# A graph-attention layer on one core: halves written straight from PSUM, second halves a step later, two turned tiles at once, remainders on GpSimd

## The chip, the core and the metric

The kernel runs on one core of one Trainium2 chip. A core has five engines that run their own instruction streams side by side: TensorE (PE in the profile; PEld are its weight loads), VectorE (DVE), ScalarE (ACT), GpSimd (POOL) and SyncE (SP). SP mainly issues DMAs; ACT and POOL can issue some as well. Every engine takes its instructions in the order in which they were issued to it. An instruction whose input isn't ready waits on a semaphore, and everything behind it on the same engine waits too. Working tiles lie in SBUF; TensorE writes its results to PSUM, whose banks hold 512 fp32 values in each of 128 partitions. A tile that is used again may be written only when all readers of its old content are done.

The metric is the device time of one execution in microseconds (us). Lower is better.

## What is computed

One pre-norm attention layer over a graph of 384 nodes with 1024 features and 16 heads of 64, all in fp32:

```python
h = jnp.maximum(_layernorm(x, axis=-1), 0.0)
q = h @ wq.T + bq ;  k = h @ wk.T + bk ;  v = h @ wv.T + bv
q2 = (q @ wiq.T + biq).reshape(N, H, D).transpose(1, 0, 2)
k2 = (k @ wik.T + bik).reshape(N, H, D).transpose(1, 0, 2)
v2 = (v @ wiv.T + biv).reshape(N, H, D).transpose(1, 0, 2)
mask = _build_mask(edge_index, edge_type, edge_type_weights, x.dtype)
scores = jnp.einsum('hnd,hmd->hnm', q2, k2) * scale + mask[None]
attn = jax.nn.softmax(scores, axis=-1)
out = jnp.einsum('hnm,hmd->hnd', attn, v2)
out = out.transpose(1, 0, 2).reshape(N, OUT_F)
return x + out @ wo.T + bo
```

The mask is a table of 384 by 384, filled from 6528 edges: minus infinity where there is no edge, the softplus of a weight by edge type where there is one.

## The kernel before

**Numbers in two parts.** To keep fp32 accuracy, an operand is held as a high part (`hi`, rounded) and a remainder (`lo`, the operand less `hi`), and a product is three matmuls into the same bank, hi·hi, hi·lo and lo·hi (`mm3`, L373 to L376, the rows L374, L375, L376 of the profile). Weights come by DMA into `raw` (`load`, L64); `split_hi` (L71, the row L81 on ACT or L79 on DVE) makes the high part and `split_lo` (L83, the row L86, on DVE or POOL) the remainder. One chunk of weights is 128 by 1024.

**Stages.** First comes the layernorm: three row tiles are normalized and turned by TensorE, eight transposes a tile in two groups of four (`ln_transpose`, L289; row L295), which ACT and DVE evict (L302, L304, L309); `warm` (L312) fills PE before that. Then come the projections v, q, iv and k, 8 chunks each of 24 matmuls. Beside them POOL and DVE build the mask table, until about 150 us.

**The fused attention loop** (L825 to L855) has 48 steps of score tiles and 11 more to drain. A step i handles score tile i, that is head i//3 and row tile i%3, at several stages of a pipeline, and issues in this order: matmuls of a filler (below), the scores `do_S(i)` (L705; two matmuls, row L711), more filler, then

- `do_ttr(i-1)` (L713, row L717, DVE): adds the mask and takes the row minimum, straight from PSUM into a tile `e`
- `do_low(i-4)` (L746, row L748, DVE) and later `do_high(i-3)` (L742, row L744, ACT), for row tile 0 of each head only (`DT = (0,)`): the normalized probabilities in fp16 as high part and remainder, which `do_turn` (L750) turns by a transposing DMA on SP's queue
- `do_exp(i-2)` (L719, row L721, ACT): exponential with its row sum
- `do_norm(i-3)` (L732): the reciprocal of the sum on DVE (L734), and for row tiles 1 and 2 the product with it on POOL (L738)
- `turns_and_av` (L777): in every third step the six transposes of row tiles 1 and 2 of a head (`turn_mm`, L755, row L758, into two PSUM banks `t`) alternate with the six matmuls of probabilities and values of the head before (`av_mm`, L769, row L773, into bank `a`)
- `do_pt` (L761), a step later, for each of the two turned tiles: ACT writes the fp16 high part (L766), DVE the remainder (L767)
- `do_ao` (L786): ACT moves one 64-partition half of the attention output (L793), DVE adds the other (L794); for each pair of heads `do_aos` (L796) splits the output into two parts, the high one on ACT (L798) and the remainder on POOL (L799)
- `run_tasks`: the head of the next chunk of the filler, and `wo_prep` (L639) in the steps of `WSTEPS`: split and load of a chunk of the output weights.

**The filler** gives PE work between the scores: `fill` (L804) takes matmuls from a list at 7.9 to 8 a step. First `fill_qk` (L610): the second projections of q and k, 16 chunks ("iq" and "ik", one pair for each two heads), which run just ahead of the heads that need them. `qk_head` (L599) starts a chunk: it evicts the previous one (`qk_done`), splits the weights of the chunk after next (its remainder on POOL for odd chunks, `PAR = 1`) and loads a further one. `qk_done` (L571) evicts a 128 by 384 result into a staging tile `nat` as high part (ACT, L384) and remainder (DVE, L385); eight DMAs for each pair of chunks then copy it by 64-partition halves into the stacks `qs` and `ks`. A stack holds, for one head, high part and remainder on top of each other, so that one matmul over 128 partitions does two of the three products, and a second one the third.

Then `fill_o` (L672): the output projection, six blocks `a` (row tile, column half), each summed over eight chunks `k` in two parts (k 0 to 3, then 4 to 7) in a bank `g` or `s`. When a part is complete, `ysum` (L660, row L663 on DVE) adds the bank to the result tile `res`. It is issued only when the bank is claimed for the next block:

```python
if k == 0:
    flush_y(1)
    oacc[OT[a]] = bank("g")
```

The order of the first part is written out by hand in `first` (L675); `wready[k]` and `6 * k + OREADY` say from which step a block may be taken.

**The end** (L862 to L874): k=7 of five blocks, each with its sum and store, then the last block in two column halves, each in a bank `t`.

`bank` (L48) takes PSUM tiles of one bank from a pool: three `g`, one `a`, two `s`, two `t`, which are all eight banks.

Of the kernel before, what the change touches and what calls it, by code (L numbers as in the profile page):

```python
# [26 lines left out]
def gnn_kernel(ctx: ExitStack, tc: tile.TileContext, x, edges, erows, etw, wq, wk, wv, wiq, wik, wiv, wo,  # L27
# [19 lines left out]

    def bank(tag):  # L48
        return psum.tile([128, 512], F32, tag=tag, name=tag, bufs={"g": 3, "a": 1}.get(tag, 2))
# [201 lines left out]
    rrow = work.tile([128, 2, N], F32R, tag="qs", name="rrow").bitcast(F32)[:, 0, :]  # L251
# [131 lines left out]
    def evac(ps, hi, lo, bias):  # L383
        nc.scalar.activation(hi, ps[:, :N], AF.Identity, bias=bias)  # L384
        nc.vector.scalar_tensor_tensor(lo, ps[:, :N], bias, hi.bitcast(F32), op0=OP.add, op1=OP.subtract)  # L385

# [75 lines left out]
    def residual(k):  # L462

        if k == 0:
            t = work.tile([128, 2, 2, N], F32R, tag="ks", name="bot")
            bob["b"] = t.bitcast(F32).rearrange("p a k n -> p (a k n)")[:, 0:D]
            nc.sync.dma_start(bob["b"], bo.partition_broadcast(128))
        if 1 <= k < 4:
            nc.sync.dma_start(xb[k - 1], x[(k - 1) * 128:k * 128, :])

    def residual_add(i):
        y = res[:, i // 2, i % 2 * 512:i % 2 * 512 + 512]
        nc.gpsimd.tensor_tensor(y, y, bob["b"][:, i % 2 * 512:i % 2 * 512 + 512], OP.add)
# [45 lines left out]
    def v2_early():  # L519
        t = work.tile([128, 2, N], F32R, tag="nat", name="tv", bufs=2)  # L520
        tv = t.bitcast(F32).rearrange("p a n -> p (a n)")[:, :512]
        nc.scalar.activation(tv, accs[5], AF.Copy)
        accs[5] = tv
# [45 lines left out]
    gps = {}  # L569

    def qk_done(w):  # L571
        n, p = chunks[w]
        q2 = nc.scalar if p == 0 else nc.sync
        nat = work.tile([128, 2, N], F32R, tag="nat", name="nat", bufs=2)
        evac(gps[w], nat[:, 0, :], nat[:, 1, :], bc[:, (3 if n == "iq" else 4) * 8 + p:(3 if n == "iq" else 4) * 8 + p + 1])
        nf = nat.bitcast(F32)
        if n == "iq":
            qs = work.tile([128, 2, N], F32R, tag="qs", name="qs")
            qf = qs.bitcast(F32)
            nc.sync.dma_start(qf[0:64, 0, :], nf[0:64, 0, :])  # L580
            q2.dma_start(qf[64:128, 0, :], nf[0:64, 1, :])
            nc.sync.dma_start(qf[0:64, 1, :], nf[64:128, 1, :])
            q2.dma_start(qf[64:128, 1, :], nf[64:128, 0, :])
            stacks["q", p] = qs
        else:
            ks = work.tile([128, 2, 2, N], F32R, tag="ks", name="ks")
            kf = ks.bitcast(F32)
            for o in range(2):
                for r in range(2):
                    (q2 if r else nc.sync).dma_start(kf[r * 64:(r + 1) * 64, o, :, :], nf[o * 64:(o + 1) * 64, :, :])  # L590
            stacks["k", p] = ks

    tasks = []
# [5 lines left out]
    def qk_head(w):  # L599
        if pendq:  # L600
            pendq.pop(0)()
        if 0 < w - W0 < NTAB:
            mask_select(w - W0)
        split_hi(w + 2)
        split_lo(w + 2, nc.gpsimd if (w + 2) % 2 == PAR else None)
        load(w + 5)
        if w == W0:
            mask_select(0)
# [21 lines left out]
    DT = (0,)  # L630
    PRE, RATE, RATE_O, RATE_E = 84, 7.9, 8, 8
    WSTEPS = (37, 40, 42, 44, 47, 51)
    PAR, OPOOL, ODVE = 1, (2, 3, 4, 6), (2,)
# [5 lines left out]
    def wo_prep(k):  # L639

        dst = None
        if k == 4:
            otile[0] = gtile("g3").rearrange("p a k n -> p (a k n)")
        if 4 <= k < 7:
            g, b = otile[0], (k - 4) * 2048
            dst = (g[:, b:b + 1024], g[:, b + 1024:b + 2048])
        split(WO + k, nc.gpsimd if k in OPOOL else None, dst, k in ODVE)
        load(WO + k + 3)
# [23 lines left out]
    def fill_o():  # L672


        first = [(0, 0), (0, 1), (1, 0), (1, 1), (2, 0), (2, 1)]  # L675
        first += [(a, k) for k in (2, 3) for a in range(3)] + [(a, k) for a in range(3, 6) for k in range(KH)]
        for a, k in first:
            while now[0] < wready[k] or now[0] < 6 * k + OREADY:
                yield 0
            if k == 0:  # L680
                flush_y(1)
                oacc[OT[a]] = bank("g")
# [5 lines left out]
        todo = [(a, k) for k in range(KH, 7) for a in range(5)]  # L688
        while todo:
# [6 lines left out]
            if k == KH:  # L696
                flush_y(1)
                oacc[OT[a]] = bank("gggss"[a])
# [3 lines left out]
    st_ps, es, sts, tps, avs, aof = {}, {}, {}, {}, {}, {}  # L702
    S = 48

    def do_S(i):  # L705
        h, t = divmod(i, 3)
        p, o = divmod(h, 2)
        qs, ks = stacks["q", p], stacks["k", p]
        ps = st_ps[i] = bank("s")
        for s in range(2):  # L710
            nc.tensor.matmul(ps[:, :N], qs[:, o, t * 128:(t + 1) * 128], ks[:, o, s, :], start=(s == 0), stop=(s == 1))  # L711

    def do_ttr(i):  # L713
        t = i % 3
        e = es[i] = work.tile([128, N], F32, tag="e", name="e", bufs=EB)
        s = sts[i] = work.tile([128, 4], F32, tag="s", name="s", bufs=12)
        nc.vector.tensor_tensor_reduce(e, st_ps.pop(i)[:, :N], ma[:, t, :], -0.125, 3.0e38, OP.add, OP.min, s[:, 0:1])  # L717

    def do_exp(i):  # L719
        s = sts[i]  # L720
        nc.scalar.activation(es[i], es[i], AF.Exp, bias=s[:, 0:1], scale=-1.0, accum_out=s[:, 1:2])  # L721
# [9 lines left out]

    def do_norm(i):  # L732
        s = sts[i]
        nc.vector.reciprocal(s[:, 2:3], s[:, 1:2])  # L734
        if i % 3 in DT:
            nc.vector.tensor_scalar(s[:, 2:3], s[:, 2:3], PSC, None, op0=OP.mult)
        else:
            nc.gpsimd.tensor_tensor(es[i], es[i], s[:, 2:3].to_broadcast([128, N]), OP.mult)  # L738

    planes = {}  # L740

    def do_high(i):  # L742
        planes[i] = plv[i // 3 % 3]
        nc.scalar.activation(planes[i][:, 0, :], es[i], AF.Copy, scale=sts[i][:, 2:3])  # L744

    def do_low(i):  # L746
        pl = planes[i]
        nc.vector.scalar_tensor_tensor(pl[:, 1, :], es.pop(i), sts[i][:, 2:3], pl[:, 0, :], op0=OP.mult, op1=OP.subtract)  # L748
# [6 lines left out]
    def turn_mm(i):  # L755
        ps = tps[i] = bank("t")
        for k in range(3):
            nc.tensor.transpose(ps[:, k * 128:(k + 1) * 128], es[i][:, k * 128:(k + 1) * 128], ident)  # L758
            yield

    def do_pt(i):  # L761
        h, t = divmod(i, 3)
        pt = ptv[h % 3]
        hi, lo = (pt[:, s * 3:s * 3 + 3, t * 128:(t + 1) * 128] for s in range(2))
        pv = tps.pop(i)[:, :N].rearrange("p (k n) -> p k n", k=3)
        nc.scalar.activation(hi, pv, AF.Copy, scale=PSC)  # L766
        nc.vector.scalar_tensor_tensor(lo, pv, PSC, hi, op0=OP.mult, op1=OP.subtract)  # L767
# [18 lines left out]
    def do_ao(h):  # L786
# [7 lines left out]
        nc.vector.scalar_tensor_tensor(aof[p][m, :], ps[m, :N], down[m], tmp[m, :], op0=OP.mult, op1=OP.add)  # L794
# [26 lines left out]
    for h in range(16):  # L821
        for t in (1, 2):
            t_at.setdefault(3 * h + 7 if h < 15 else 3 * h + 5 + t, []).append(3 * h + t)
        a_at[3 * h + 10 if h < 15 else 3 * h + 9] = h
    for i in range(S + 11):  # L825
# [8 lines left out]
        if 0 <= i - 4 < S and (i - 4) % 3 in DT:  # L834
# [3 lines left out]
        if 0 <= i - 3 < S:  # L838
            do_norm(i - 3)
            if (i - 3) % 3 in DT:  # L840
                do_high(i - 3)
        turns_and_av(t_at.get(i, []), [a_at[i]] if i in a_at else [])
        for x in t_at.get(i - 1, []):
            do_pt(x)
        if i - 1 in a_at:
            do_ao(a_at[i - 1])
        if a_at.get(i - 2, 0) % 2:
            do_aos(a_at[i - 2])
        run_tasks()
        if 0 <= i - 4 < S and (i - 4) % 3 in DT:  # L850
            do_turn(i - 4)
        if i in WSTEPS:
            wo_prep(wp)
            wready[wp] = i + 2
            wp += 1  # L855
    while gens:
# [57 lines left out]
```

## Time and profile before

| what | value |
|---|---|
| median of 3 runs | 296.02 us (294.78 to 296.08) |
| the profiled execution | 294.56 us, span 292.8 us |
| granted TensorE clock | 1.00 |
| PE busy | 284.7 us, 97% of the span, 1610 matmuls |
| VectorE busy | 208.2 us, 71% |
| ScalarE busy | 159.7 us, 55% |
| GpSimd busy | 154.8 us, 53% |
| from 180 to 200 us: PE, VectorE, ScalarE, GpSimd busy | 20.00, 15.13, 16.51, 10.65 us |
| from 250 to 260 us: PE busy | 8.88 of 10 us |
| stacks filled by SP's DMAs (q2 and k2) | 30 of 96 KB and 30 of 192 KB |

The span is the time from the first to the last instruction seen by the profiler; the 1.76 us beside it lie around it. A line of the timeline or of the groups gives a start or a total, a duration, the engine, the line of the code, the operation, output and inputs with their shapes, how often, and in brackets how long the engine had been idle and for whom. A line of the waits says which instruction of which engine waited for which, in all, how many times, and the longest. PE's matmul records overlap (the ends are modelled), so the distance between two starts is the better measure of what a matmul costs.

From 184 to 206 us the heads follow each other at equal distance: the transposes of successive heads start at 185.63, 192.49 and 199.33 us.

### The profile page before, as it was taken

Reading aid. Unit: us, or ns where it says so; the run is one execution under the profiler, and the core shown is the slowest. Engines: PE = TensorE matmul, PEld = TensorE weight load, DVE = VectorE, ACT = ScalarE, POOL = GpSimd, SP = SyncE. Lnnn points to the kernel's source line nnn. Section 1 sums busy time; section 2 is a strip of 40 time slices with the busy share of each in tenths; the row PEclk is TensorE's granted clock in tenths of the full one; section 3 lists DMA queues with packets and bytes.
Section 4 is the critical chain, followed back from the end, with each engine's and each line's share of the span. In section 5 each row is a group of like instructions: output and inputs, shape, how many; then the busy total and the mean of one; then the engine's idle time right before and its main releaser. Section 6 shows DMA issues by size and latency. Waiting matters only on the chain. (4 is left out here: it accounts for less than half of the span.)

```text
span 292.8 us, 4859 instructions
## 1 busy us (share of the span) xinstructions
PE 284.7 (97%) x1610; PEld 267.4 (91%) x1610; DVE 208.2 (71%) x509; ACT 159.7 (55%) x291; POOL 154.8 (53%) x153
## 2 busy tenths in 40 slices
PE   6999999999999999999999999999999999989995
PEld 5999999999988889999999999999999998868874
DVE  3858996667665452999966768878786876788623
ACT  3894543244331222343643778787878788766510
POOL 3765576437775787992004256262627268636210
PEclk9999999999999999999999999999999999999999
DMA  7799857973463342278438879879797969901105
GB/s 268 248 321 404 292 209 254 323 242 112 143 189 122 121 146 72 72 224 296 154 86 227 241 208 211 212 166 227 166 234 147 254 133 234 230 2 27 27 3 215
DMA packets 33305, 54.60 MB, mean 187 GB/s; under 512 B 17408, under 2 KB 20992, under 8 KB 33280
## 3 DMA queue, kind: packets, MB, share of 16 engines
q1 hardware_dynamic: 30896, 51.90, 61.4%
q0 software_dynamic: 2064, 1.80, 2.2%
q10 hardware_dynamic: 320, 0.59, 0.8%
q8 instruction: 13, 0.21, 0.3%
q14 instruction: 12, 0.10, 0.1%
HBM read 38.30 MB, written 3.39 MB: 142 GB/s over the span
## 5 line engine op out<-in xcount | busy, mean ns | idle before, releaser
L374 PE MATMUL g<-g,whl 128*128 128x384 f32 x312 | 105.8, 339 | 0.0
L376 PE MATMUL g<-g,whl 128*128 128x384 f32 x312 | 104.3, 334 | 0.0
L375 PE MATMUL g<-g,whl 128*128 128x384 f32 x312 | 104.2, 334 | 0.0
L231 POOL DMA_INDIRECT tab<-val,idx x51 | 59.7, 1171 | 32.0 <-issue 11.8
L81 ACT ACTIVATE whl<-raw 128x1024 fp32r<-128x1024 f32 x51 | 53.5, 1050 | 29.8 <-PE g L376 21.1
L86 DVE TENSOR_TENSOR whl<-raw,whl 128x1024 fp32r<-128x1024 f32 x41 | 53.8, 1313 | 20.1 <-ACT whl L81 17.0
L374 PEld LDWEIGHTS g<-g,whl 128*128 128x128 f32 x312 | 58.6, 188 | 0.2
L375 PEld LDWEIGHTS g<-g,whl 128*128 128x128 f32 x312 | 58.6, 188 | 0.0
L376 PEld LDWEIGHTS g<-g,whl 128*128 128x128 f32 x312 | 58.6, 188 | 0.1
L390 ACT ACTIVATE g<-f,bc 128x384 fp32r<-128x384 f32 x24 | 14.8, 618 | 53.7 <-DVE f L389 44.8
L738 POOL TENSOR_TENSOR e<-e,s 128x384 f32<-128x384 f32 x32 | 26.4, 829 | 31.2 <-DVE s L734 23.0
L86 POOL TENSOR_TENSOR whl<-raw,whl 128x1024 fp32r<-128x1024 f32 x11 | 26.3, 2395 | 25.9 <-ACT whl L81 25.0
L721 ACT ACTIVATE e<-e,s 128x384 f32<-128x384 f32 x48 | 29.1, 607 | 2.0 <-DVE s L717 1.2
L717 DVE CUSTOM_DVE_ANT_0 e<-s,ma 128x384 f32<-128x384 f32 x48 | 26.4, 552 | 4.3 <-PE s L711 3.7
L389 DVE TENSOR_TENSOR f<-g,rrow 128x384 f32<-128x384 f32 x24 | 13.3, 554 | 18.0 <-PE g L376 18.0
L773 PE MATMUL a<-pt,vhl 128*128 128x384 f16 x96 | 26.1, 326 | 0.0
L758 PE MATMUL t<-ident,e 128*128 128x128 f32 x96 | 24.9, 272 | 0.0
L711 PE MATMUL s<-ks,qs 128*128 128x384 f32 x96 | 24.5, 335 | 0.0
L767 DVE SCALAR_TENSOR_TENSOR pt<-t,pt 128x384 f16<-128x384 f32 x32 | 16.6, 549 | 8.2 <-ACT pt L766 8.2
L799 POOL TENSOR_TENSOR g<-aof,g 128x384 fp32r<-128x384 f32 x8 | 8.3, 1041 | 25.5 <-ACT g L798 25.5
L711 PEld LDWEIGHTS s<-ks,qs 128*128 128x128 f32 x96 | 17.5, 188 | 0.9
L744 ACT ACTIVATE pt<-e,s 128x384 f16<-128x384 f32 x16 | 9.9, 616 | 15.4 <-issue 9.4
(166 smaller groups left out, 447.0 us busy)
## 6 DMA issues: line engine op xcount, KB each, us to landing
ks<-nat SPq DMA_DIRECT2D x30, 192.0 KB
raw<-in_wv_dram SPq DMA_DIRECT2D x8, 512.0 KB
raw<-in_wq_dram SPq DMA_DIRECT2D x8, 512.0 KB
raw<-in_wiv_dram SPq DMA_DIRECT2D x8, 512.0 KB
raw<-in_wk_dram SPq DMA_DIRECT2D x8, 512.0 KB
raw<-in_wiq_dram SPq DMA_DIRECT2D x8, 512.0 KB
raw<-in_wik_dram SPq DMA_DIRECT2D x8, 512.0 KB
raw<-in_wo_dram SPq DMA_DIRECT2D x8, 512.0 KB
```

The costliest lines, as they stand in the source:

```text
L81: nc.scalar.activation(dst[0], raw[w], AF.Copy)
L86: (eng or nc.vector).tensor_tensor(lo, raw[w], hi.bitcast(F32), OP.subtract)
L231: nc.gpsimd.indirect_dma_start(out=tabs[c // RNG], out_offset=bass.IndirectOffsetOnAxis(ap=idx[:, c:c + 1], axis=0), in_=val[:, c:c + 1], ...
L374: nc.tensor.matmul(ps, lhi, rhi, start=first, stop=False)
L375: nc.tensor.matmul(ps, lhi, rlo, start=False, stop=False)
L376: nc.tensor.matmul(ps, llo, rhi, start=False, stop=last)
L711: nc.tensor.matmul(ps[:, :N], qs[:, o, t * 128:(t + 1) * 128], ks[:, o, s, :], start=(s == 0), stop=(s == 1))
L717: nc.vector.tensor_tensor_reduce(e, st_ps.pop(i)[:, :N], ma[:, t, :], -0.125, 3.0e38, OP.add, OP.min, s[:, 0:1])
L721: nc.scalar.activation(es[i], es[i], AF.Exp, bias=s[:, 0:1], scale=-1.0, accum_out=s[:, 1:2])
L738: nc.gpsimd.tensor_tensor(es[i], es[i], s[:, 2:3].to_broadcast([128, N]), OP.mult)
L758: nc.tensor.transpose(ps[:, k * 128:(k + 1) * 128], es[i][:, k * 128:(k + 1) * 128], ident)
L773: nc.tensor.matmul(ps[:, :N], vhl[:, k, h, :, :], ptv[h % 3][:, 3 * s + k, :], start=(k == 0 and s == 0), stop=(k == 2 and s == 1))
```

## The change

- **One PSUM tile for the turned tiles.** The two banks `t` become one tile `turn` of two banks. `bank("t")` gives its halves in turn. `turn_mm` writes both turned tiles of a head side by side into it, and `do_pt` evicts both with one instruction on ACT and one on DVE (head 15, whose tiles are turned in two steps, keeps two).
- **Stacks from PSUM.** `qk_done` writes the two 64-partition halves of q2 and k2 from PSUM into the stacks, high part by ACT and remainder by DVE, each half by itself. The staging tile and its DMAs go. Only the high part of k2, which is needed on both halves of the partitions, is copied by a DMA, one for each head; the unused quarter of the k stacks is set to zero once, by POOL.
- **VectorE's second halves a step later.** The remainders of `qk_done` and `do_pt`, the second half of `do_ao` and those remainders of the output weights that are on DVE go to a list `later`, which is run in the next step just behind `do_ttr`. `do_aos` comes a step later too, and the loop has one step more.
- **Remainders on GpSimd.** The remainders of all second-projection chunks (and of the first two chunks of the output weights) go to POOL.
- **Output projection.** `flush_y` runs at the end of every step. `first` takes the blocks k = 0, 1 of the first three banks and then k = 2, 3 of them bank by bank, `todo` takes block 2 after 3 and 4, and two entries of `WSTEPS` are earlier (36 and 38 for 37 and 40).
- The row sums and factors of a head lie in one small tile, with some generality that is not used (`LAG = 0`).

```diff
+    turn = psum.tile([128, 2, 512], F32, tag="t", name="t", bufs=1)
+    nturn = itertools.count()
+
     def bank(tag):
-        return psum.tile([128, 512], F32, tag=tag, name=tag, bufs={"g": 3, "a": 1}.get(tag, 2))
+        if tag == "t":
+            return turn[:, next(nturn) % 2, :]
+        return psum.tile([128, 512], F32, tag=tag, name=tag, bufs={"g": 3, "a": 1, "s": 2}[tag])
...
+    ksb = [[work.tile([128, 2, N], F32R, tag=f"ks{o}", name="ks") for j in range(2)] for o in range(2)]
+    for o in range(2):
+        for j in range(2):
+            nc.gpsimd.memset(ksb[o][j].bitcast(F32)[64 - o * 64:128 - o * 64, 1, :], 0.0)
 
     def qk_done(w):
         n, p = chunks[w]
-        q2 = nc.scalar if p == 0 else nc.sync
-        nat = work.tile([128, 2, N], F32R, tag="nat", name="nat", bufs=2)
-        evac(gps[w], nat[:, 0, :], nat[:, 1, :], bc[:, (3 if n == "iq" else 4) * 8 + p:(3 if n == "iq" else 4) * 8 + p + 1])
...
+        for o in range(2):
+            m, l = slice(o * 64, o * 64 + 64), slice(64 - o * 64, 128 - o * 64)
+            if n == "iq":
+                t = work.tile([128, N], F32R, tag=f"qs{o}", name="qs", bufs=2 + o)
+                hi, lo = t[m, :], t[l, :]
+            else:
+                t = ksb[o][p % 2]
+                hi, lo = t[m, 0, :], t[m, 1, :]
+            stacks[n, p, o] = t
+            nc.scalar.activation(hi, ps[m, :N], AF.Identity, bias=bias[m])
+            halves.append((m, hi, lo))
+            if n == "ik":
+                kf = t.bitcast(F32)
+                (nc.scalar if p == 0 and o else nc.sync).dma_start(kf[l, 0, :], kf[m, 0, :])
+        for m, hi, lo in halves:
+            later.append(lambda m=m, hi=hi, lo=lo: nc.vector.scalar_tensor_tensor(
+                lo, ps[m, :N], bias[m], hi.bitcast(F32), op0=OP.add, op1=OP.subtract))
+        if now[0] < 0:
+            run_later()
...
-        split_hi(w + 2)
-        split_lo(w + 2, nc.gpsimd if (w + 2) % 2 == PAR else None)
+        split_hi(w + 2, dve=(w + 2) % 2 == PAR)
+        eng = nc.gpsimd
+        if eng is None and now[0] >= 0:
+            later.append(lambda: split_lo(w + 2))
+        else:
+            split_lo(w + 2, eng)
...
-    WSTEPS = (37, 40, 42, 44, 47, 51)
-    PAR, OPOOL, ODVE = 1, (2, 3, 4, 6), (2,)
+    WSTEPS = (36, 38, 42, 44, 47, 51)
+    PAR, OPOOL, ODVE = 9, (2, 3, 4, 6), (2,)
...
-        split(WO + k, nc.gpsimd if k in OPOOL else None, dst, k in ODVE)
+        split_hi(WO + k, dst, k in ODVE)
+        if k in OPOOL:
+            split_lo(WO + k, nc.gpsimd)
+        else:
+            later.append(lambda: split_lo(WO + k))
...
-        first = [(0, 0), (0, 1), (1, 0), (1, 1), (2, 0), (2, 1)]
-        first += [(a, k) for k in (2, 3) for a in range(3)] + [(a, k) for a in range(3, 6) for k in range(KH)]
+        first = [(a, k) for c in (0, 2) for a in range(3) for k in (c, c + 1)]
+        first += [(a, k) for a in range(3, 6) for k in range(KH)]
...
             if k == 0:
-                flush_y(1)
                 oacc[OT[a]] = bank("g")
...
-        todo = [(a, k) for k in range(KH, 7) for a in range(5)]
+        todo = [(a, k) for k in range(KH, 7) for a in (0, 1, 3, 4, 2)]
...
     def turn_mm(i):
-        ps = tps[i] = bank("t")
+        h, t = divmod(i, 3)
+        ps = turn.rearrange("p b n -> p (b n)")
         for k in range(3):
-            nc.tensor.transpose(ps[:, k * 128:(k + 1) * 128], es[i][:, k * 128:(k + 1) * 128], ident)
+            nc.tensor.transpose(ps[:, k * 256 + (t - 1) * 128:k * 256 + t * 128], es[i][:, k * 128:(k + 1) * 128], ident)
             yield
...
+    def do_pt(x):
+        h, t = divmod(x[0], 3)
+        c = slice(t * 128, (t + len(x)) * 128)
+        hi, lo = (ptv[h % 3][:, s * 3:s * 3 + 3, c] for s in range(2))
+        pv = turn.rearrange("p b n -> p (b n)")[:, :768].rearrange("p (k n) -> p k n", k=3)[:, :, c.start - 128:c.stop - 128]
         nc.scalar.activation(hi, pv, AF.Copy, scale=PSC)
-        nc.vector.scalar_tensor_tensor(lo, pv, PSC, hi, op0=OP.mult, op1=OP.subtract)
+        later.append(lambda: nc.vector.scalar_tensor_tensor(lo, pv, PSC, hi, op0=OP.mult, op1=OP.subtract))
...
-        nc.vector.scalar_tensor_tensor(aof[p][m, :], ps[m, :N], down[m], tmp[m, :], op0=OP.mult, op1=OP.add)
+        dst = aof[p][m, :]
+        later.append(lambda: nc.vector.scalar_tensor_tensor(dst, ps[m, :N], down[m], tmp[m, :], op0=OP.mult, op1=OP.add))
...
-    for i in range(S + 11):
+    for i in range(S + 12):
...
             do_ttr(i - 1)
+        run_later()
...
-        if a_at.get(i - 2, 0) % 2:
-            do_aos(a_at[i - 2])
+        if a_at.get(i - 3, 0) % 2:
+            do_aos(a_at[i - 3])
...
+        flush_y()
```

## The prediction, made before the changed kernel was run

> **What bounds the kernel now.** I read the page first. Its rows of busy time and of slices say that TensorE works 97% of the span and is short of full only in the first slice and near the end:
>
> ```profile
> PE 284.7 (97%) x1610; PEld 267.4 (91%) x1610; DVE 208.2 (71%) x509; ACT 159.7 (55%) x291; POOL 154.8 (53%) x153
> PE   6999999999999999999999999999999999989995
> ```
>
> No other engine is near that, and the granted clock is 1.00 in every stretch. The change issues the same matmuls (1610 rows) in almost the same order, so it can move the end only through the moments in which PE stands still. The view of waits lists them for PE, longest in total first:
>
> ```profile
> PE s L295 <- ACT g L283: 1.5, 1, 1.5
> PE g L315 <- POOL ident masks.py:199: 1.4, 1, 1.4
> PE g L374 <- DVE res L663: 1.4, 1, 1.4
> PE g L295 <- DVE g L287: 0.4, 1, 0.4
> ```
>
> Three of the four are in the layernorm at the start. The third lies in the attention phase, and the timeline there tells what it is:
>
> ```profile
> 258.27 1.23 DVE L86 TENSOR_TENSOR g<-raw,g 128x1024 fp32r<-128x1024 f32 x1 [0.46 <-ACT g L81]
> 258.37 0.51 PE L711 MATMUL s<-ks,qs 128*128 128x384 f32 x2
> 259.51 0.69 DVE L663 TENSOR_TENSOR res<-g,res 128x512 f32<-128x512 f32 x1
> ...
> 260.25 0.50 PE L374 MATMUL g<-whl,g 128*128 128x512 f32 x1 [1.37 <-DVE res L663]
> ```
>
> The output projection needs a bank that ysum (L663) must empty. ysum was only issued when the bank was claimed, and stood on DVE behind a weight remainder (L86) of 1.23 us, which itself had waited for ACT. The second L711 started about 0.17 after 258.37, the next matmul at 260.25: 1.71 between starts that lie 0.17 apart elsewhere, so 1.54 us is lost. Then I read the starts of the other PE rows from 21 us on: outside this place, and 0.11 at 283.33, they follow each other at their own rates.
>
> **The change, part by part.**
>
> *The bank.* flush_y now runs at the end of every step, and the blocks for k=2,3 of bank 0 come before those of bank 1, so the first sum is issued at step 41 and its bank claimed at 43. A step is a third of a head, 6.84/3 = 2.28 us; two steps are 4.56, against 0.69 for ysum and at most the 1.23 of a remainder that may stand before it. The whole 1.54 goes; if DVE is 2.6 us late, it stays. Term: -1.54, bounds -1.54 and 0. wo_prep moves with it (steps 36 and 38 for 37 and 40; hi, remainder on POOL and one 512 KB load each). Transposes of step 19 start at 199.33, so step 38 runs from 242.6 to 244.9; its hi (1.05) and remainder (2.39) then end by 246.0 to 248.3, and k=3 is first read in step 41, at 249.5: 1.2 or more hide it.
>
> *The second use of one PSUM tile, at the start.* The two t banks are now halves of one tile, and the order of the changed program with its waits shows two new PE waits outside the attention. In the layernorm the four transposes of the second t half must now also wait for ACT's eviction of the first:
>
> ```profile
> 8.60 0.59 ACT L302 ACTIVATE g<-t 128x512 fp32r<-128x512 f32 x1
> 8.95 0.60 PE L295 MATMUL t<-ident,g 128*128 128x128 f32 x4
> 9.65 0.59 ACT L302 ACTIVATE g<-t 128x512 fp32r<-128x512 f32 x1
> 10.12 1.16 ACT L351 ACTIVATE whl<-raw 128x512 fp32r<-128x512 f32 x2
> ```
>
> The eviction ends at 9.19, so with about 0.1 for the release the transposes start at 9.25 to 9.30 instead of 8.95. They end 0.60 later, at 9.9; ACT, which began at 9.65, follows 0.3 later, then L351, the split that the first projection matmul (10.81) waits for. That is +0.3 on the path. Bounds: 0, if L351 is taken first or PE waits for DVE's transposed half anyway, and 0.35. I take +0.3.
>
> *The same, at the tail.* The last tile is made in two column halves, each in a t bank:
>
> ```profile
> 287.85 0.28 PE L374 MATMUL t<-g,g 128*128 128x256 f32 x1
> ...
> 288.05 0.42 DVE L663 TENSOR_TENSOR res<-t,res 128x256 f32<-128x256 f32 x1 [0.74 <-PE t L376]
> ...
> 289.48 0.42 DVE L663 TENSOR_TENSOR res<-t,res 128x256 f32<-128x256 f32 x1 [1.01 <-PE t L376]
> ```
>
> The matmul at 287.85 opens the second half while the first half's sum has not begun. After, it waits for that sum: 288.05 + 0.42 = 288.47, plus 0.05 (the release at 260.20 to 260.25 above) to 0.13. That is 0.67 to 0.75 later, and the twelve matmuls, the sum at 289.48 and the last store all follow. Term +0.7; nothing hides it, since no other matmul is left.
>
> *Halves of q2 and k2.* Per chunk (16 of them) ACT does two 64x384 (nearest row L793, 0.67; issue distance about 0.5) for one 128x384 (0.57), DVE two of 0.62 (L794) for one. So +0.5 to +0.7 for ACT and +0.62 for DVE. The staging DMAs (8 a pair) become 2, which frees SP's queue; PE never waited for a stack, so that gains nothing. A stack is read three or more steps after its eviction (7 us), which hides both.
>
> *Turned tiles at once.* For 15 heads, ACT does one of 768 columns instead of two L766 (0.86 a pair), DVE one instead of two L767 (1.00 a pair): by 1.05/1024 and (0.69-0.42)/256 a column about 0.8 and 0.95. Even. But with one tile, the next head's first transpose waits for DVE's remainder. The remainder now runs one step later, behind the next ttr: S ends at 188.84, ttr by 189.45, remainder by 190.4, and the transpose is due at 192.49. 2.1 us hide it.
>
> *Remainders on GpSimd and later.* Half of the chunks' L86 leave DVE (1.23 each) for POOL (2.39 each). POOL per head goes from two L738 (1.66), half an L799 (0.52) and half an L86 (1.20), 3.4 us, to 4.6 of 6.84. DVE's later second halves save it standing: in the head groups it idled 8.2 us for ACT's pt (L766). All of this is off the path while POOL's second norm comes before its transposes:
>
> ```profile
> 192.99 0.82 POOL L738 TENSOR_TENSOR e<-e,s 128x384 f32<-128x384 f32 x1
> 194.01 2.39 POOL L86 TENSOR_TENSOR whl<-raw,whl 128x1024 fp32r<-128x1024 f32 x1 [0.20 <-ACT whl L81]
> 196.36 0.83 POOL L738 TENSOR_TENSOR e<-e,s 128x384 f32<-128x384 f32 x1
> ```
>
> That norm ends at 197.19; its head's transposes start at 199.33, and those of this tile three pairs of 0.27 later, at 200.14. Of these 2.95, the extra ACT half takes up to 0.5 (it stands before the split that L86 needs) and L799, now a step later, up to 0.43: 2.0 left. Cost 0.
>
> Sum: -1.54 + 0.3 + 0.7 = -0.54 on the profiled execution's 294.56 (span 292.8 and 1.76 around it): 294.0. That execution lies 1.46 under the median of the runs, 296.02, whose lowest is 294.78; the same difference on the median gives 295.5, 0.2% less. A change under 0.5% (1.48 us) I call none, since the runs of one kernel spread that far.
>
> **A rule against the change.** One row of this trace shows DVE held by POOL:
>
> ```profile
> 267.88 1.75 DVE L748 SCALAR_TENSOR_TENSOR pt<-e,s,pt 128x384 f16<-128x384 f32 x1 [0.24 <-ACT pt L744]
> 266.82 2.40 POOL L86 TENSOR_TENSOR g<-raw,g 128x1024 fp32r<-128x1024 f32 x1 [2.08 <-ACT g L81]
> ```
>
> L748 reads two tiles in SBUF, takes 0.62 elsewhere, and here ended 0.4 after POOL's L86; rows with one input in PSUM (L717, L767, L663) keep 0.55 to 0.69 beside L86. The Trainium skill, "SBUF — State Buffer", section "Who interferes with whom", has it as a rule: a VectorE instruction with two SBUF inputs and a GpSimd one that reads SBUF exclude each other for a whole instruction. The trace agrees. POOL now has an L86 in every head, so the two can meet in every head: 1.75 - 0.62 = 1.13 each time, which the 2.0 above still hides, so one meeting a head leaves the sum as it is and two (2.26) bring the late POOL below. Against that, L86 comes behind the first norm, whose reciprocal stands behind L748 on DVE, so that they rarely meet.
>
> **The rivals.**
> *Faster: the new PSUM waits are hidden.* If the first projection matmul waits for something else (the raw weights, DVE's half of the layernorm) and the tail's half is released early, the sum is -1.54, with the 0.11 that the matmul at 283.33 waits for POOL -1.65: 294.4 against the median. For it: the page's chain of waits is nearly all PE, with no start-up ACT step in it. Against: the tail has no other work.
>
> *Slower: POOL becomes late.* Place: L86 between the two norms. From the point where it ends more than 2.0 us later than now, the second tile's transposes wait, in order, with every matmul behind them. If L86 takes double (held by DVE as L748 was held), 2.39 - 2.0 = 0.4 a head for 14 to 15 heads, +5.7, with the sum above +5.1: 301.1; at half of that overrun 298.3. For it: POOL at 67% and three instructions deep per head. Against: POOL's two groups of L86 have means of 2.395 and 2.392, beside a DVE that is over 70% busy.
>
> *Slower: the single turned tile.* If ACT (5.7 of 6.84 us a head by my count, against 5.3) is late with the turned tile by more than 2.1 us, where evictions, split and exp fall together, PE waits a few tenths a head: 0.2 by 15 is +3.0, in all 298.5. For it: ACT idles only 0.3 before exp in the steady phase. Against: 1.1 us a head is still spare.
>
> *It does not do what it says:* the sums come early but DVE is still late, because remainders now pile up behind ttr. Then the 1.54 stays and the costs come: +1.0, 297.0.
>
> **How the numbers follow.** My forecast 0.42, the hidden waits 0.28, late POOL 0.11, late turned tile 0.11, the stall kept 0.08. Predicted 295.5. Its own range is 294.3 to 296.4 (the spread of the runs and the bounds of the three terms). To hold 8 in 10 it must take in the hidden waits with the spread of the runs (294.4 less about 1), and the stall kept and most of the milder slow cases: 293.4 to 298.7. Faster by over 0.5% is the hidden waits and a little of the forecast, 0.30; same, 0.42; slower, 0.28 (the two late cases, and the kept stall in part).
>
> **What would show it.** In the changed profile: the wait on DVE's res of 1.4 at about 260 gone; a new PE wait for ACT at about 9.2, with the first projection matmul near 11.1; a new PE wait on DVE's res of about 0.7 in the last three microseconds; POOL's 128x1024 remainders 19 instead of 11, each still 2.4. I am wrong if PE shows repeated waits on POOL's e or DVE's pt before the transposes, or if heads are further apart than 6.84 us.

## The result, and the profile after

Both kernels ran 18 times. The changed one took 295.95 us in the median (295.18 to 296.86), the one before 294.64 (294.34 to 296.25); the ratio is 1.0037, 95% interval [1.0023, 1.0051]. The forecast was -0.2%; it came out 0.4% slower. The profiled execution took 295.35 us with a span of 293.6, that is 0.8 more than before, where the prediction's sum said 0.54 less.

The page after, the same rows as before (busy time by engine, then PE's tenths in 40 slices):

```profile
PE 286.1 (97%) x1610; PEld 267.6 (91%) x1610; DVE 214.8 (73%) x502; ACT 170.2 (58%) x292; POOL 174.3 (59%) x165
PE   6999999999999999999999999999999998999994
```

PE has the same 1610 matmuls. POOL has 19.5 us more, ACT 10.5. The view of PE's waits after:

```profile
PE g L320 <- POOL ident masks.py:199: 1.4, 1, 1.4
PE s L300 <- ACT g L288: 0.9, 1, 0.9
PE g L379 <- DVE ks L596: 0.6, 1, 0.6
PE t L379 <- DVE res L684: 0.5, 1, 0.5
PE s L730 <- DVE s L738: 0.3, 1, 0.3
PE g L300 <- DVE g L292: 0.3, 1, 0.3
PE t L300 <- ACT g L307: 0.2, 1, 0.2
```

The wait of 1.4 for the sum (L663, now L684) in the middle of the output projection is gone, as forecast. The two from the shared PSUM tile are there, at the start (the last line) and at the tail (`PE t`). But two more lines are new: a matmul L379 that takes a bank g waits for L596, the remainder of k2, and the scores L730 wait for the row minimum L738. Both lie in one place; these are the rows of PE, DVE and POOL that matter there, out of the timeline of the changed kernel:

```profile
241.08 0.70 DVE L84 CAST whl<-raw 128x1024 fp32r<-128x1024 f32 x1
241.70 0.55 DVE L738 CUSTOM_DVE_ANT_0 e<-s,ma 128x384 f32<-128x384 f32 x1
241.91 2.39 POOL L91 TENSOR_TENSOR whl<-raw,whl 128x1024 fp32r<-128x1024 f32 x1 [0.69 <-PE t L793]
242.18 2.55 DVE L782 SCALAR_TENSOR_TENSOR pt<-e,s,pt 128x384 f16<-128x384 f32 x1
244.75 0.40 PE L381 MATMUL g<-whl,g 128*128 128x512 f32 x1
244.87 0.56 DVE L738 CUSTOM_DVE_ANT_0 e<-s,ma 128x384 f32<-128x384 f32 x1
245.35 1.24 DVE L596 SCALAR_TENSOR_TENSOR ks<-g,bc,ks 64x384 fp32r<-64x384 f32 x2
245.49 0.61 PE L730 MATMUL s<-ks,qs 128*128 128x384 f32 x2 [0.34 <-DVE s L738]
246.74 0.47 PE L379 MATMUL g<-whl,g 128*128 128x512 f32 x1 [0.64 <-DVE ks L596]
```

L782, the remainder of row tile 0's probabilities, takes 2.55 us where it takes 0.62 elsewhere (185.41, for one), and ends 0.4 after POOL's L91 (241.91 + 2.39 = 244.30). That L91 is the remainder of chunk 2 of the output weights, from `wo_prep` at the end of step 36. Its high part is the cast L84 on DVE, so that POOL starts when the cast is done (241.08 + 0.70 = 241.78; L91 at 241.91), and the next step on DVE begins with L738 and L782. Behind the held L782 stand the next row minimum and then the remainder that frees the bank. On PE the starts 244.75, 245.49 and 246.74 are 0.74 and 1.25 apart; with 0.23 for a 512-column matmul and 0.17 + 0.17 for the two score matmuls it would be 0.23 and 0.34. So 0.5 + 0.9 = 1.4 us are lost.

The two forecast costs are these rows, the first projection matmul and the first matmul of the last half block:

```profile
11.14 2.10 PE L424 MATMUL g<-g,whl 128*128 128x256 f32 x16
288.68 0.39 PE L379 MATMUL t<-g,g 128*128 128x256 f32 x1 [0.52 <-DVE res L684]
```

The sum of the terms as the trace has them: -1.54 for the stall that went, +0.33 at the start (11.14, before at 10.81), +0.68 at the tail (288.68; at the pace of the matmuls before it, it would have started at 288.00), +1.4 here. That is +0.9; the spans differ by 0.8.

Both kernels' times fall into two groups 1.3 to 1.5 us apart: of the 18, the changed kernel has nine up to 295.46 and nine from 296.44, the kernel before fifteen up to 295.0 and three from 296.02. In the changed kernel, of which each group has a trace, what parts them lies in the first 13 us (last section). Both kernels have both groups, so below the lower groups are compared as well: medians 295.35 after, 294.45 to 294.56 before, 0.8 to 0.9 apart, as the two spans are.

### The profile page after: what moved, and what is told of

It is laid out like the page before. It is cut to its first block, busy times and chain, and to the rows that moved or that the text cites. A ratio compares the mean times of both kernels' runs of the same rounds, so it can differ in the third digit from the quotient of the medians.

```text
span 293.6 us, 4773 instructions
## 1 busy us (share of the span) xinstructions
PE 286.1 (97%) x1610; PEld 267.6 (91%) x1610; DVE 214.8 (73%) x502; ACT 170.2 (58%) x292; POOL 174.3 (59%) x165
## 5 line engine op out<-in xcount | busy, mean ns | idle before, releaser
L379 PE MATMUL g<-g,whl 128*128 128x384 f32 x312 | 105.8, 339 | 0.0
L381 PE MATMUL g<-g,whl 128*128 128x384 f32 x312 | 104.4, 335 | 0.0
L236 POOL DMA_INDIRECT tab<-val,idx x51 | 57.8, 1132 | 34.1 <-issue 9.9
L86 ACT ACTIVATE whl<-raw 128x1024 fp32r<-128x1024 f32 x51 | 53.8, 1054 | 25.2 <-PE g L381 21.1
L91 POOL TENSOR_TENSOR whl<-raw,whl 128x1024 fp32r<-128x1024 f32 x19 | 46.3, 2438 | 29.9 <-ACT whl L86 29.3
L379 PEld LDWEIGHTS g<-g,whl 128*128 128x128 f32 x312 | 58.6, 188 | 0.2
L381 PEld LDWEIGHTS g<-g,whl 128*128 128x128 f32 x312 | 58.6, 188 | 0.2 <-POOL whl L91 0.2
L91 DVE TENSOR_TENSOR whl<-raw,whl 128x1024 fp32r<-128x1024 f32 x33 | 44.1, 1337 | 15.5 <-ACT whl L86 15.5
L738 DVE CUSTOM_DVE_ANT_0 e<-s,ma 128x384 f32<-128x384 f32 x48 | 26.7, 556 | 7.6 <-PE s L730 6.2
L743 ACT ACTIVATE e<-e,s 128x384 f32<-128x384 f32 x48 | 29.0, 605 | 0.3
L808 PE MATMUL a<-pt,vhl 128*128 128x384 f16 x96 | 26.1, 326 | 0.0
L730 PE MATMUL s<-ks,qs 128*128 128x384 f32 x96 | 24.6, 336 | 0.3 <-DVE s L738 0.3
L802 DVE SCALAR_TENSOR_TENSOR pt<-t,pt 128x768 f16<-128x768 f32 (+1 forms) x17 | 15.5, 909 | 6.5 <-ACT pt L801 6.4
L730 PEld LDWEIGHTS s<-ks,qs 128*128 128x128 f32 x96 | 17.4, 188 | 1.6 <-DVE s L738 0.8
L392 DVE SCALAR_TENSOR_TENSOR g<-f,bc,g 128x384 fp32r<-128x384 f32 x24 | 16.7, 700 | 0.7 <-ACT g L391 0.7
L778 ACT ACTIVATE pt<-e,s 128x384 f16<-128x384 f32 x16 | 9.9, 617 | 11.0 <-ACT e L743 6.6
```

Source lines behind the costliest of these rows:

```text
L86: nc.scalar.activation(dst[0], raw[w], AF.Copy)
L91: (eng or nc.vector).tensor_tensor(lo, raw[w], hi.bitcast(F32), OP.subtract)
L236: nc.gpsimd.indirect_dma_start(out=tabs[c // RNG], out_offset=bass.IndirectOffsetOnAxis(ap=idx[:, c:c + 1], axis=0), in_=val[:, c:c + 1], ...
L379: nc.tensor.matmul(ps, lhi, rhi, start=first, stop=False)
L381: nc.tensor.matmul(ps, llo, rhi, start=False, stop=last)
L730: nc.tensor.matmul(ps[:, :N], qs[:, t * 128:(t + 1) * 128], ks[:, s, :], start=(s == 0), stop=(s == 1))
```

## Experiments

Three theories were set against each other for the new stall. *Held once*: the collision of L782 and L91 makes it. *Drift*: ACT and DVE wait for each other in a loop that takes longer than PE's 6.84 us a head, so that DVE was late already. (The row minimum, `do_ttr`, is L738 in the changed kernel; how long after its scores it starts is called its lag below.) *Bank kept*: the remainder L596, deferred by a step, holds the bank. The trace gives a reason for the second one. This is the last PSUM reader that the transposes of a head wait for (L802), twice, with the transposes themselves, in the timeline of the changed kernel:

```profile
182.94 0.95 DVE L802 SCALAR_TENSOR_TENSOR pt<-t,pt 128x768 f16<-128x768 f32 x1
185.97 0.27 PE L793 MATMUL t<-ident,e 128*128 128x128 f32 x1
...
239.43 0.96 DVE L802 SCALAR_TENSOR_TENSOR pt<-t,pt 128x768 f16<-128x768 f32 x1 [0.49 <-ACT pt L801]
240.91 0.27 PE L793 MATMUL t<-ident,e 128*128 128x128 f32 x1
```

L802 ends at 183.89 and the transposes start at 185.97, so there are 2.1 us to spare, which is what the prediction had; eight heads later 240.91 - 240.39 = 0.5. This time to spare is called the cover below. The hold of L782, 2.55 - 0.62 = 1.93, less this cover is 1.4, as much as PE lost; that the two have to agree is not shown.

**The changed kernel again** (no edit).

> The changed kernel once more, unaltered. In its first trace TensorE stood still for 1.33 us between 244.7 and 246.8 (0.5 before the scores L730, 0.1 between them, 0.8 before the matmul L379 that takes a bank from L596), while VectorE's L782 took 2.55 us instead of 0.62 beside a GpSimd remainder. Its 18 times fall into two groups, 8 of 295.2 to 295.5 and 10 of 296.4 to 296.9, and that trace is of the lower one. Theory 'held once' (the one collision of L782 with L91 makes the stall): a trace of the upper group shows L782 held at more places, or longer. Theory 'drift' (ACT and DVE wait for each other in a loop that is longer than TensorE's 6.84 us a head, so that VectorE falls some 0.2 us further behind with each head, which the first trace shows: ttr starts 0.3 us after its scores at 179 us and 2.6 at 236): a trace of the upper group shows several further waits of 0.1 to 0.5 of the turns L793 and the products L808 for DVE before 245 us, adding up to about 1.3.

Ten times of 295.2 to 295.7 and two of 296.6 and 296.8; ratio to before 1.0015 [0.9996, 1.0034]. The trace is of the upper group, 1.4 us longer in its span. Neither theory's picture of that group came true: the same L782 is held for 2.54, the stall at 245 has the same two waits, and no further ones follow; the whole difference is at the start. The expectation above puts the stall at 1.33 and the groups at 8 and 10; by the rows it is 1.4, and nine and nine.

**The remainder of chunk 2 one step later** (e6).

```diff
         if k in OPOOL:
-            split_lo(WO + k, nc.gpsimd)
+            k > 2 and split_lo(WO + k, nc.gpsimd)
...
-        flush_y()
+        flush_y(); i == 37 and split_lo(WO + 2, nc.gpsimd)
```

> Only the GpSimd remainder of wo chunk 2 is issued one step later, so that it comes behind two norms on GpSimd and no longer beside VectorE's L782 of step 37; all other engines have the same order. 'Held once': L782 is 0.62 throughout, the stall of 1.33 at 245 goes down to 0.1 or less, 1.2 to 1.3 us faster than the changed kernel, so 0.1 or 0.2 slower than before at most. 'Drift': the lag of ttr behind the scores still grows to 2.5 at 236, the products L808 still start with 0.1 us to spare at 241, some waits of 0.1 to 0.5 stay, and the gain is between 0.5 and 1.3. 'Bank kept by the deferred remainder' (L596 of the last chunk, run a step late, holds the bank): the wait of L379 for L596 stays at 0.5 or more.

Ratio to before 0.9988 [0.9967, 1.0009], six times of 293.77 to 293.95 and six above 295; the lower group is 1.5 below that of the changed kernel. In its trace L782 of that step takes 0.61, ahead of the moved L91, and PE's waits have neither L596 nor L738:

```profile
242.16 0.61 DVE L782 SCALAR_TENSOR_TENSOR pt<-e,s,pt 128x384 f16<-128x384 f32 x1
243.77 2.41 POOL L91 TENSOR_TENSOR whl<-raw,whl 128x1024 fp32r<-128x1024 f32 x1
```

The lag stayed: L738 starts 2.6 after its scores at 236, and the products L808 have 0.1 to spare at 241. A later L782 is held here (1.51 at 248.36, against the expectation's 0.62 throughout), which costs PE nothing; the cover of that head is 1.2. So without the collision the drift alone costs nothing yet, and a deferred L596 alone doesn't hold the bank.

**Second halves behind the reciprocal** (e7).

```diff
             do_ttr(i - 1)
-        run_later()
...
+        run_later()
         turns_and_av(t_at.get(i, []), [a_at[i]] if i in a_at else [])
```

> The deferred second halves of VectorE run behind the low half and the reciprocal of the step instead of ahead of them; nothing else moves, and the collision's two instructions keep their order. 'Drift': ScalarE no longer waits for the reciprocal behind second halves, the lag of ttr at 236 is 1 us or less (2.6 in the changed kernel), the turns L793 start with 1.5 us or more to spare up to 241 (0.5 in the changed kernel), and the stall at 245 is 0.4 or less even if L782 is held, so 0.9 to 1.3 us faster than the changed kernel. 'Held once': L782 still takes about 2.5 and the stall stays at 1 or more, the time within 0.3 of the changed kernel.

Ratio 0.9975 [0.9958, 0.9993]; the lower group is at 293.88, 1.5 below that of the changed kernel. The timeline of this kernel at the same place:

```profile
238.64 0.95 DVE L802 SCALAR_TENSOR_TENSOR pt<-t,pt 128x768 f16<-128x768 f32 x1
240.95 2.38 POOL L91 TENSOR_TENSOR whl<-raw,whl 128x1024 fp32r<-128x1024 f32 x1 [0.68 <-issue]
241.22 2.53 DVE L782 SCALAR_TENSOR_TENSOR pt<-e,s,pt 128x384 f16<-128x384 f32 x1
242.09 0.27 PE L793 MATMUL t<-ident,e 128*128 128x128 f32 x1
```

The collision is as before, 2.53 us, and yet PE has no wait there: L802 ends at 239.59, 2.5 before the transposes, and L738 starts 0.5 after its scores at 235, not 2.6. The groups of ACT from 186 to 234 us show what closed the loop; the last columns are the idle time ahead of the row and for whom. First the changed kernel, then this one:

```profile
L778 ACT ACTIVATE pt<-e,s 128x384 f16<-128x384 f32 x6 | 3.7, 617 | 3.4 <-ACT e L743 3.4
```

```profile
L778 ACT ACTIVATE pt<-e,s 128x384 f16<-128x384 f32 x7 | 4.2, 601 | 0.0
L590 ACT ACTIVATE ks<-g,bc 64x384 fp32r<-64x384 f32 x8 | 4.6, 576 | 2.9 <-PE g L381 2.8
```

In the changed kernel ACT idles 3.4 us ahead of L778, the high part of row tile 0, and hardly elsewhere. The view names ACT's own L743, but L778 also needs the factor from DVE (L767 and L769), and that comes later, as the timeline of the changed kernel shows:

```profile
210.37 0.81 ACT L801 ACTIVATE pt<-t 128x768 f16<-128x768 f32 x1
211.21 0.96 DVE L802 SCALAR_TENSOR_TENSOR pt<-t,pt 128x768 f16<-128x768 f32 x1 [0.49 <-ACT pt L801]
212.09 0.60 DVE L830 SCALAR_TENSOR_TENSOR aof<-a,vsc,aot 64x384 f32<-64x384 f32 x1
212.79 0.15 DVE L769 TENSOR_SCALAR s<-s 128x1 f32<-128x1 f32 x1
213.03 0.62 ACT L778 ACTIVATE pt<-e,s 128x384 f16<-128x384 f32 x1 [0.42 <-ACT e L743]
```

The loop runs from ACT's L801 to DVE's deferred L802, which waits for it, over L830 to the reciprocal and the factor (L769 ends at 212.94), and back to ACT's L778 at 213.03. With the reciprocal first, ACT waits for almost nothing but PE (L381): it keeps pace with PE.

**The remainders of q2 and k2 at once** (e2).

```diff
-            later.append(lambda m=m, hi=hi, lo=lo: nc.vector.scalar_tensor_tensor(
-                lo, ps[m, :N], bias[m], hi.bitcast(F32), op0=OP.add, op1=OP.subtract))
-        if now[0] < 0:
-            run_later()
+            nc.vector.scalar_tensor_tensor(lo, ps[m, :N], bias[m], hi.bitcast(F32), op0=OP.add, op1=OP.subtract)
```

> The two VectorE remainders of q2 and k2 (L596) are issued at once, in the step of their ScalarE halves, and no longer deferred. 'Bank kept by the deferred remainder': the wait at 246 for L596 goes, the stall at 245 is 0.5 or less and the kernel 0.8 or more faster than the changed one. 'Held once' and 'drift': the bank comes free about 0.5 sooner but the minimum of the scores (L738) is 1.2 later, so the stall stays at 1 or more and moves from L379 to the scores L730; within 0.4 of the changed kernel, or slower, since VectorE again stands waiting for ScalarE at the head of each chunk.

Ratio 1.002 [1.0003, 1.0037], median 295.51 against 295.35. The wait for L596 is gone, but PE now waits for L738, in three places (0.3 at 224, 0.3 at 238, 0.6 at 246 by the distances of the starts), not for 1 us or more in the one place, as was expected. The sum, 1.2, is nearly the old 1.4, so a bank that a deferred remainder keeps was not the cause. L782 is held here too (2.52); the cover at 242 is 1.5, and less is lost behind the collision.

**The weights' high parts of every second chunk on DVE** (e8).

```diff
-    PAR, OPOOL, ODVE = 9, (2, 3, 4, 6), (2,)
+    PAR, OPOOL, ODVE = 1, (2, 3, 4, 6), (2,)
```

> The changed kernel, with the high part of every second chunk's weights made by VectorE (the row L84, 0.70) instead of ScalarE (L86, 1.06): ScalarE has about 0.5 us less a head, VectorE 0.35 more, GpSimd the same. 'Drift by ScalarE's load': the loop of ScalarE and VectorE gets shorter than 6.84 us, ttr is 1.5 us late at most at 236 (2.6 in the changed kernel), the stall of 1.33 at 245 falls to 0.4 or less, and the time by 0.9 to 1.3. Rival: VectorE's second halves ahead of the reciprocal set the loop, VectorE's extra 0.35 undoes the gain, and the lag and the stall stay as they are.

Ratio 0.9985 [0.9967, 1.0002]; lower group 293.83, 1.5 below the changed kernel. L738 starts 1.4 after its scores at 234, the transposes at 241 have 2.7 us to spare, L782 takes 2.53 and no stall follows. So the loop can be shortened at ACT as well as at DVE.

**The start and the tail** (e3, e4).

```diff
-            ps = bank("st"[half] if t < 2 else "ga"[half])
+            ps = bank(("st", "sg", "ga")[t][half])
```

> The changed kernel, with the second group of turned columns of the layernorm's second tile in a bank g of its own instead of the other half of the one t tile. If the prediction's term of +0.3 at the start is right, these four transposes start at 8.95 again instead of 9.30, without a wait for ScalarE's eviction, and in an execution whose transposes run at 0.11 us each the first projection matmul starts near 10.8 instead of 11.14: 0.3 faster than the changed kernel, everything else unchanged (the stall of 1.33 at 245 stays, the wait of 0.68 at the tail too). Rival: the path there is set by VectorE's or ScalarE's other work, and the first projection matmul stays at 11.1.

Ratio 1.0011 [0.9992, 1.003]; lower group 295.06, 0.3 below the changed kernel. Its trace is of the upper group, in which the changed kernel doesn't wait for L307 either, and the first projection matmul comes equally late in both (12.62, and 12.61 in the changed kernel's second trace), so it shows nothing of the gain. The two times of the upper group, 296.8, are no lower than the changed kernel's. The trace of e11, which has the same bank, does show it: from the second group of transposes (7.71) to the first projection matmul (11.16) it takes 3.45 us, as in the kernel before (7.36 to 10.81), against 3.80 in the changed kernel (7.34 to 11.14).

```diff
-        oacc[OT[5]] = bank("t")
+        oacc[OT[5]] = bank("ta"[c[0] > 0])
```

> The changed kernel, with the second column half of the last tile in bank a, which is free by then. If the term of +0.7 at the tail is right, PE's wait for the first half's sum goes, the twelve matmuls follow at 0.12 us each, and the kernel is 0.7 faster than the changed one. Rival: the end is set by the stores on SP's queue, and the gain is under 0.3.

Ratio 1.0019 [0.9999, 1.0039], in which seven of twelve times are of the upper group; lower group 294.59, 0.76 below the changed kernel, and the upper ones 295.99 against 296.63. In the trace the second half's first matmul starts 0.12 after the last of the first half. Both terms were right, the one at the start in executions of the lower group.

**The output projection alone, in the kernel before** (e9).

```diff
-    WSTEPS = (37, 40, 42, 44, 47, 51)
+    WSTEPS = (36, 38, 42, 44, 47, 51)
...
+        first = [(a, k) for c in (0, 2) for a in range(3) for k in (c, c + 1)]
+        first += [(a, k) for a in range(3, 6) for k in range(KH)]
...
             if k == 0:
-                flush_y(1)
...
             wp += 1
+        flush_y()
```

> The kernel before with nothing but the change's output-projection part: sums at the end of each step, k=2,3 bank by bank, the earlier steps 36 and 38. The prediction's term of -1.54 alone: the stall of 1.53 at 260 goes. 'Drift needed': here the turns have 2.8 us or more to spare all the time, so the cast and remainder of wo chunk 2 may hold L748 for up to 2.5 us and no wait over 0.3 follows on TensorE; 1.2 to 1.6 faster than before. 'Held once': the same collision makes a stall of about 1.3 and the time is within 0.4 of before.

Ratio 0.9947 [0.9926, 0.9968]. The timeline of this kernel shows the same collision, and its view of PE's waits, which is complete here, shows no wait after the layernorm (L423 is the first projection matmul):

```profile
238.71 0.68 DVE L79 CAST whl<-raw 128x1024 fp32r<-128x1024 f32 x1
239.53 2.38 POOL L86 TENSOR_TENSOR whl<-raw,whl 128x1024 fp32r<-128x1024 f32 x1 [0.90 <-issue]
239.78 2.54 DVE L748 SCALAR_TENSOR_TENSOR pt<-e,s,pt 128x384 f16<-128x384 f32 x1
```

```profile
PE g L315 <- POOL ident masks.py:199: 1.4, 1, 1.4
PE s L295 <- ACT g L283: 1.0, 1, 1.0
PE g L423 <- ACT whl L351: 0.3, 1, 0.3
```

The stall at 260 is gone from the trace, and the lower groups differ by 1.4 (293.1 against 294.46). A collision of the same size cost nothing where the transposes have 3.3 us to spare (those at 240.66). In the kernel before no L748 between 172 and 264 us is held, so the earlier step alone brings the collision.

**All three repairs** (e10: the edits of e7, e3 and e4 in one).

> The changed kernel with all three repairs: second halves behind the reciprocal, a bank g at the start, a bank a at the tail. If the terms add up, 1.4 + 0.3 + 0.7 = 2.4 faster than the changed kernel, about 1.6 faster than before (ratio 0.9945), TensorE without any wait over 0.2 after the layernorm. If the start or the tail is set by something else, 0.3 or 0.7 less.

Ratio 0.9946 [0.9925, 0.9967]; lower group 293.02, 2.3 below the changed kernel, and PE's waits end with the first projection matmul. The terms add up (2.4 was expected). It is hardly faster than e9 (293.1), which leaves q2 and k2, the turned tiles and the remainders as they were: of the whole change only the output projection brought time that the runs can tell from none.

**A longer fill at the start** (e11: e10 with `WARM = (26, 6, 0)` for `(20, 6, 0)`).

> The kernel with all three repairs (e10), with 26 instead of 20 transposes of the identity ahead of the first layernorm tile. In all nine traces so far TensorE stands still for 1.2 to 1.8 us between those transposes and the first real ones at 6.8; its transposes go from one each 0.213 us to one each 0.109 at a moment that differs between executions: at 4.3 in the first trace of before, at 6.8 in others (lower group of times), and only at 10.0 to 10.9 in the four traces of the upper group, which is 1.3 us longer. If that standing still delays the doubling, six more transposes (1.28 us) fill the gap, the first real ones start at 6.9 at the latest, the doubling comes before 7 in every execution, and the upper group is gone: 12 times of 292.6 to 293.5, none over 294.2. If the moment is set by something else, 2 to 6 of 12 times are still 294.3 or more. If the fill runs over the moment when the data is ready, all times are 0.1 to 0.3 longer.

Six times of 292.75 to 293.2, ratio to before 0.9938 [0.992, 0.9957], the lowest median of all. No time is of the upper group, but with six of them that may be chance (e2 had none in twelve). The expectation's moments were missed: the first real transposes start at 7.05 and the doubling comes at about 7.4, not before 7. (In the first trace of before it comes at 4.8 by the rows, not 4.3.) The rest of what the trace shows is in the last section.

## Why the prediction was wrong

*The stall at the bank, -1.54*: right. It is gone in the changed kernel, and alone its removal gave -1.4 (e9).

*The start, +0.3, and the tail, +0.7*: right, measured +0.33 and +0.68 in the trace, 0.3 and 0.76 in the times of e3 and e4.

*"L86 comes behind the first norm, whose reciprocal stands behind L748 on DVE, so that they rarely meet"*: this failed. It held for the chunks of q2 and k2, whose L91 come where the text says: between 172 and 264 us only the one L782 at 242.18 takes over 1 us. It left out the remainder of chunk 2 of the output weights. The prediction did look at the moved `wo_prep`, but only at when its result is ready, not at what its instructions hold up on the way: its cast on DVE at the end of step 36 releases POOL's L91 right ahead of the L782 of step 37. One meeting took 1.93 us (2.55 - 0.62), not the 1.13 that the row of before had; the rule that the prediction took from the Trainium skill ("SBUF — State Buffer", "Who interferes with whom") agrees with it: L782 began 0.3 after L91, L748 in the row of before 1.1 after L86, and both ended 0.4 after POOL's instruction.

*"2.1 us hide it" and "1.1 us a head is still spare"*: this failed too, and it is why the meeting reached PE. The 2.1 were right at 186 us, but were taken for every head. Free time on ACT was not a reserve, since ACT spent it waiting for DVE's reciprocal while DVE waited for ACT's evictions. By the two pairs of rows above, the cover shrank from 2.1 to 0.5 over eight heads, 0.2 a head. With a cover of 2.5 us or more the hold of 1.9 costs nothing (e7, e8, e9), and without the hold the small cover suffices (e6). Shown: either of the two repairs removes the whole 1.4; it takes both causes to make the stall.

*The rivals*: the late turned tile named the right place for its cause (ACT and DVE late with what the transposes need), but expected tenths on every head; nothing was paid until the one hold. Late POOL did not happen: PE has no wait for a norm, and 19 L91 have a mean of 2.44. The prediction's signs of being wrong, repeated waits of PE on POOL's e or DVE's pt, did not appear either; the loss came as waits for L738 and L596, behind the one hold.

Without the +1.4 the sum has the sign that was forecast; with it, the other. That the 295.5 lies close to the measured 295.95, and inside the wide range, is luck: it was taken off a median of three runs, 296.02, two of which were of the upper group, and 18 runs of the same kernel have 294.64.

## What to carry to other kernels

Before a second half is moved behind the next step's work, look at which small instruction stands behind it on its new place and who waits for that; a reciprocal on which another engine waits goes first. Time to spare that was measured in one head counts only if it is the same several heads later, so compare the loop through two engines with the pace of the engine that bounds the kernel, not the busy time of each. And of a step that is moved, ask also what its instructions hold up beside which others, not only when its result is ready.

## What the runs showed of the hardware

In the changed kernel the two groups of times come from the start. Rows of PE in its first trace (lower group) and in its second (upper group):

```profile
7.34 0.60 PE L300 MATMUL t<-ident,g 128*128 128x128 f32 x4
7.78 0.88 PE L320 MATMUL g<-ident 128*128 128x128 f32 x6
```

```profile
7.67 1.06 PE L300 MATMUL t<-ident,g 128*128 128x128 f32 x4
8.52 1.49 PE L320 MATMUL g<-ident 128*128 128x128 f32 x6
9.80 1.06 PE L300 MATMUL s<-ident,g 128*128 128x128 f32 x4
10.66 0.74 PE L300 MATMUL t<-ident,g 128*128 128x128 f32 x4
11.24 0.60 PE L300 MATMUL g<-ident,g 128*128 128x128 f32 x4
...
12.61 0.38 PE L424 MATMUL g<-g,whl 128*128 128x256 f32 x1 [0.33 <-ACT whl L356]
```

Four transposes take 1.06 where they take 0.60 in the other trace, that is one each 0.213 us instead of 0.109, until 10.9 us; the first projection matmul comes at 12.61 instead of 11.14. In all four traces of the upper group (a0, e3, e7, e10) this doubling of the rate comes at 10 us or later, in all others by 7.6; no execution of the kernel before that is of the upper group was traced. The granted clock reads 0.998 to 1.0 in either, so that column doesn't show it. The Trainium skill, "TensorE: Matmul & The Clock Gate", section "Part 1: The HAM clock gate (the "warmup" mystery)", says that the clock doubles after a busy window of some 3.4 us whose phase is free, so that the moment varies between runs; the traces agree that it varies, and by more than the half microsecond given there (from 4.8 us in the kernel before to 10.9 here). That the doubled rate is this clock is not shown by any run here. In the changed kernel PE is idle for 0.9 us ahead of the first real transposes at 6.84. In e11, where that gap is filled, they begin with 0.83 for four and go on with 0.60:

```profile
1.44 5.81 PE L320 MATMUL g<-ident 128*128 128x128 f32 x26 [1.44 <-POOL ident masks.py:199]
7.05 0.83 PE L300 MATMUL s<-ident,g 128*128 128x128 f32 x4
7.71 0.60 PE L300 MATMUL t<-ident,g 128*128 128x128 f32 x4
```

Whether the filled gap always prevents the late doubling stays open with six runs. For the comparison it matters that a late doubling costs 1.3 us here, about as much as most of the edits: the changed kernel had half its 18 runs in the upper group, the kernel before a sixth, which is some of the 0.4%. In its next twelve runs the changed kernel had two, so the half may be chance.
